# Linear attention with a router on one core: the recurrence's small matmuls in one burst for both sequences, sums of squares later, gates in two steps, the last tile in halves

## The chip, the core and the metric

The kernel runs on one core of a Trainium2 chip. The core has five engines that run on their own, each with a queue that it works off in order: TensorE (PE) multiplies matrices into PSUM, VectorE (DVE), ScalarE (ACT) and GpSimd (POOL) work on tiles, and SyncE (SP) issues most of the DMA transfers. PE's weight loads (loads of the operand that stays in the array) have a row of their own in the profile, PEld. PSUM has eight banks per partition; one bank holds 512 float32 values. The metric is the device time of one execution in microseconds.

## The reference

The input x has 4 sequences of 512 tokens with 512 features. It is normalised and goes two ways.

```
xn = layernorm(x)
# s: attention without softmax, 16 heads of 128, in blocks of tokens
q, k, v = silu(xn @ w_qkv)
kv      = decay * kv + (k * k_decay)^T @ v           # a state per head
o       = (q * q_decay) @ kv + ((q @ k^T) * mask) @ v
s       = (sigmoid(xn @ w_gate) * norm_w * o * rsqrt(mean(o*o) + eps)) @ w_out
# g: softmax router over 64 experts, the 8 largest weights
g       = silu(xn * sum(top8) + top8 @ expert_bias)
out     = x + s * g
```

The mean of o*o runs over all 16 heads (2048 values) of a token.

## The kernel before

**Products.** All large products are float32 products made of three passes over a high and a low part of each operand (`PASSES`): ACT casts the high part, POOL or DVE subtracts it to get the low part. Each matmul has a 128x128 stationary tile and 512 moving columns. The head products (q, k and gates) of two sequences at a time use a scheme with seven block products instead of eight (`unit`, lines 478 to 516). So a *unit* has seven steps of six matmuls. Behind each step come its additions on DVE, the sigmoid on ACT, a product on DVE that is put off to the next step (`deferred`), and then all that the list `after[i]` holds for step i. These lists are how the order of the work is written: nothing is scheduled by a tool.

**Stages.** First the v products (lines 919 to 971), stored to DRAM. Then 48 units in two passes over pairs of sequences (p = 0, 1; `todo`, from line 1005): for each two heads a gate unit, then the q and k unit of either head. Last the output projection (from line 1071): 64 steps, one for each sequence and head, of 12 matmuls (4 token tiles, 3 passes), accumulated over the 16 heads in four PSUM banks `po`.

**The recurrence.** A head's attention runs in the unit after its q and k unit, for the pair's two sequences b1 and b0 (`attention`, line 717). It has three parts, all made of small float32 matmuls (each is one or two records of 128 columns in the trace):

- `scores_qk` (line 660): scores `sa` = k q, transposed k `kt`; then DVE masks the scores (`at`), ACT scales k (`kd`) and POOL scales q (`qd`).
- `states` (line 684): `ss` = kd v, then ACT copies the first block and DVE adds the running state (`st`).
- `attend` (line 697): `o` from at v and qd st; DVE makes y = o * norm_w * gate and SP stores it; ACT squares o, and POOL adds the squares over the heads into `sqs`.

Before, these stand behind the steps one sequence at a time: scores of b1 behind step 1, of b0 behind step 2, states behind 3 and 4, output of b1 behind 5, and of b0 behind step 0 of the next unit. The outputs use two pools of PSUM: `ps_o` (one bank) for b1, `ps_sc` (three banks, for all that is small) for b0. The last unit's k for b0 is the last of four results of a unit; its product with the sigmoid is put off to step 0 of the next unit.

**Routing.** From unit 3 on, the router's small steps (`routing`, line 339) are dealt out one to a step, seven in a unit. Most of them are DVE operations.

**Around the projection.** `sum_squares` (line 726) sums `sqs` over partitions with matmuls of one column, then POOL raises to -1/2. For the first pair it stands behind step 4 of a unit in the second pass; for the second pair, behind step 3 of the projection. The last head's attention runs at steps 0 to 2 of the projection (`last_steps`, line 1058). `ahead` (line 982) loads y and w_out some steps ahead and splits them two or three steps ahead, at the start of every step. `ffn` (line 752) makes the router's gate for one token tile: DVE normalises x, PE multiplies the top-8 weights by the bias (`pu`), then DVE adds, ACT takes the sigmoid and POOL multiplies. `finish` (line 788) multiplies the projection by the norm and the gate, adds x, and stores.

Of the kernel before, what the change touches and what calls it, by code (L numbers as in the profile page):

```python
# [8 lines left out]
F32 = mybir.dt.float32  # L9
# [5 lines left out]
P = 128  # L15
NH = 16
# [34 lines left out]
def kernel(  # L51
# [44 lines left out]
    def tok(b, t):  # L96
        return bass.ds(b * N + t * P, P)
# [443 lines left out]
    def nothing():  # L541
        return [[] for _ in PRODUCTS]
# [114 lines left out]

    def scores_qk(b, h, attp):  # L660
        s, d = (b, h), dec[b // PB, h]
        q, k = chunks(qs[s]), chunks(ks[s])
        pa = ps_sc.tile([P, NT, P], F32, tag="sc", name=f"sa_{b}_{h}")
        for c in range(NT):
            nc.tensor.matmul(pa[:, c], k[:, c], q[:, c], start=True, stop=True)  # L665
        pk = ps_sc.tile([P, NT - 1, P], F32, tag="sc", name=f"kt_{b}_{h}")
        for c in range(NT - 1):
            nc.tensor.transpose(pk[:, c], k[:, c], ident)  # L668
        at[s] = attp.tile([P, NT, P], F32, tag="at", name=f"at_{b}_{h}")
        nc.vector.tensor_tensor(  # L670
            at[s], pa, d[:, 0, None, :].to_broadcast([P, NT, P]), ALU.mult
        )
        kd[s] = attp.tile([P, NT - 1, P], F32, tag="kd", name=f"kd_{b}_{h}")
        nc.scalar.activation(kd[s], pk, AF.Copy, scale=kdecay[:, h : h + 1])  # L674
        qd[s] = attp.tile([P, NT - 1, P], F32, tag="qd", name=f"qd_{b}_{h}")
        nc.gpsimd.tensor_tensor(  # L676
            qd[s], q[:, 1:], d[:, 1, None, :].to_broadcast([P, NT - 1, P]), ALU.mult
        )
# [18 lines left out]
    def attend(b, h, attp, psum=(ps_o, "o")):  # L697
        s = (b, h)
        po = psum[0].tile([P, N], F32, tag=psum[1], name=f"o_{b}_{h}")
        for c in range(NT):  # L700
            o = chunks(po)[:, c]
            nc.tensor.matmul(o, v_of(b, h, c), at[s][:, c], start=True, stop=(c == 0))  # L702
            if c > 0:
                nc.tensor.matmul(o, st[s][:, c - 1], qd[s][:, c - 1], start=False, stop=True)  # L704
        y = attp.tile([P, N], F32, tag="y", name=f"y_{b}_{h}")
        nc.vector.scalar_tensor_tensor(y, po, nw[:, h : h + 1], gts[s], ALU.mult, ALU.mult)  # L706
        nc.sync.dma_start(out=y_d[s], in_=y)
        if h == 0:
            sq[b] = attp.tile([P, N], F32, tag="sqs", name=f"sqs_{b}")
            nc.scalar.activation(sq[b], po, AF.Square)  # L710
        else:
            s1 = attp.tile([P, N], F32, tag="sqt", name=f"sq_{b}_{h}", bufs=1)
            nc.scalar.activation(s1, po, AF.Square)  # L713
            nc.gpsimd.tensor_tensor(sq[b], sq[b], s1, ALU.add)  # L714


    def attention(p, h, attp):
        b0, b1 = p * PB, p * PB + 1
        f = lambda g, b: [lambda: g(b, h, attp)]
        now = [  # L720
            [], f(scores_qk, b1), f(scores_qk, b0), f(states, b1), f(states, b0), f(attend, b1), [],
        ]
        return now, [lambda: attend(b0, h, attp, (ps_sc, "sc"))]


    def sum_squares(b):
# [25 lines left out]
    def ffn(b, t, outp):  # L752
        u = outp.tile([P, F], F32, tag="u", name=f"u_{b}_{t}")
        normalise(u, xts[b, t], b, t)
        pu = ps_sc.tile([P, F], F32, tag="sc", name=f"pu_{b}_{t}")
        for i in range(2):
            nc.tensor.matmul(pu, wT[b][:, t, :], ebs[0][:, i, :], start=(i == 0), stop=(i == 1))  # L757
        nc.vector.scalar_tensor_tensor(u, u, sumw[b][:, t : t + 1], pu, ALU.mult, ALU.add)
        sg = wk.tile([P, F], F32, tag="sg", name=f"sgu_{b}_{t}")
        nc.scalar.activation(sg, u, AF.Sigmoid)  # L760
        nc.gpsimd.tensor_tensor(u, u, sg, ALU.mult)  # L761
        gates[b, t] = u
# [22 lines left out]
        split_lo(nc.gpsimd, wr[:, 1], w, wr[:, 0])  # L785
        wos[h] = wr

    def finish(b, t, ps):
        u, xt = gates[b, t], xts[b, t]
        last = b == B - 1  # L790
        nc.vector.scalar_tensor_tensor(u, ps, rms[b][:, t : t + 1], u, ALU.mult, ALU.mult)  # L791
        (nc.vector if last else nc.gpsimd).tensor_tensor(u, u, xt, ALU.add)
        (nc.scalar if last and t % 2 else nc.sync).dma_start(out=out[tok(b, t), :], in_=u)

    def o_head(pos, h, yr, t):
        for n, (wi, yi) in enumerate(PASSES):
            nc.tensor.matmul(  # L797
                pos[t], yr[:, yi, bass.ts(t, P)], wos[h][:, wi],
                start=(h == 0 and n == 0), stop=(h == NH - 1 and n == len(PASSES) - 1),
            )  # L800


# [202 lines left out]
    for i, (p, kind, n, w) in enumerate(todo):  # L1005
        after = nothing()
        for j, f in enumerate(later):
            after[min(4 * j, 6)].append(f)
        later = []
        if i + 2 < len(todo):  # L1010
            todo[i + 2][3].load()()
        if i + 1 < len(todo):
            weight_steps(todo[i + 1][3], after)
        if pending is not None:
            now, later = attention(*pending, attp)
            for j, fs in enumerate(now):
                after[j] += fs
            if pending[1] == NH - 1:
                later.append(lambda: [sum_squares(b) for b in range(PB)])
            pending = None  # L1020
        if i >= 3:
            for j in range(len(PRODUCTS)):
                if route_steps and (len(route_steps) > 1 or j):
                    after[j].append(route_steps.pop(0))
        if nu - len(XN) + NX <= i < nu:
            if xc is None:
                rb_stack.close()
                xc = right(ha_stack, "xc")
            m = i - (nu - len(XN) + NX)
            block(1, m, xc, m)  # L1030
            load_block(1, m)
        if i == nu - 1:
            for m in range(NX):
                def again(m=m):
                    block(1, len(XN) - NX + m, xa, m)
                    load_block(1, len(XN) - NX + m)
                after[m].append(again)
        if i == nu:
            xb_stack.close()
            op = left(o_stack, "o", 2)  # L1040
        if i == len(todo) - 1:
            ahead(0, 2, 0)
            after[3].append(lambda: ahead(0, 2, 1))
            after[5].append(lambda: ahead(0, 3, 2))
        if kind == "g":
            gate_unit(p, n, w, attp, after)
        else:
            qk_unit(p, n, w, attp, after)
            pending = (p, n)
            if n + 1 < NH or p + 1 < NP:  # L1050
                nxt = (p, n + 1) if n + 1 < NH else (p + 1, 0)
                load_v(*nxt, attp)
                load_decay(*nxt, attp)
# [5 lines left out]
        [lambda: scores_qk(b1, hl, attp), lambda: scores_qk(b0, hl, attp)],  # L1059
        [lambda: states(b1, hl, attp), lambda: states(b0, hl, attp)],  # L1060
        [lambda: attend(b1, hl, attp), lambda: attend(b0, hl, attp, (ps_sc, "sc"))],
        [lambda: sum_squares(b0), lambda: sum_squares(b1)],
    ]

    late_stack = ExitStack()
# [4 lines left out]
        f()  # L1070
    for i, (b, h) in enumerate(steps):
        last = b == B - 1
        if i == len(last_steps) - 1:
            ha_stack.close()
            hw_stack.close()
            late = right(late_stack, "late", 5)
        if late is None:
            ahead(i, 3, 2)
        else:
            ahead(i, 6, 3)  # L1080
        if h == 0:
            for t in range(NT):
                pos[t] = ps_mm.tile([P, F], F32, tag="mm", name=f"po_{b}_{t}")
        if not last or h < NH - TAIL:
            yr = parts.pop(0)
            for t in range(NT):
                o_head(pos, h, yr, t)
                if h == NH - 1:
                    finish(b, t, pos[t])
        elif h == NH - 1:  # L1090
            for t in range(NT):
                for k, yr in enumerate(parts[0:TAIL]):
                    o_head(pos, NH - TAIL + k, yr, t)
                finish(b, t, pos[t])
        if i < len(last_steps):
            for f in last_steps[i]:
                f()
        if late is not None:
            if i == 3:
                load_eb(late)  # L1100
            if i == 5:
                split_eb(late)
            m = h - (4 if b == 0 else 0)
            if m == 0:
                load_wT(b, late)
            if 0 <= m < NT:
                load_x(late, b, m)
            if m in (3, 5, 7, 9):
                ffn(b, (m - 3) // 2, late)
    late_stack.close()  # L1110
    o_stack.close()

# [42 lines left out]
```

## Time and profile before

| | us |
|---|---|
| median of 3 runs | 1075.56 (1074.61 to 1075.66) |
| profiled execution, its own time | 1074.7 |
| its span, first to last instruction | 1073.0 |
| PE busy, 5762 matmuls | 1058.8 |
| PEld busy | 909.6 |
| POOL busy | 724.2 |
| DVE busy | 686.3 |
| ACT busy | 479.8 |

The largest groups of PE are the head products (line 496), the projection (line 797: 768 matmuls, 180.0 us busy) and the small matmuls of the recurrence (lines 665 to 704). The mean granted clock of PE is 0.998.

How to read it: the busy time of PE counts overlapping matmuls once, and the end of a matmul is modelled, so 99% does not say that the array works at its peak. Better is the time from the start of one matmul to the start of the next. In the timelines, a row gives the start in us from the span's start, the duration in us, the engine, the line, the operation, output<-inputs, the number of instructions merged into the row, and in brackets the idle time of the engine ahead of it with what ended it. In the list of waits a row gives who waited for whom, the total in us, how many times, and the longest.

### The profile page before, as it was taken

How to read it: one execution, taken by the hardware profiler on the slowest of the kernel's cores; microseconds unless marked ns; L12 is line 12 of the kernel's file. 1: busy time of each engine (PE TensorE's matmuls, PEld its weight loads, DVE VectorE, ACT ScalarE, POOL GpSimd, SP SyncE). 2: the span in 40 equal slices, each digit the busy share in tenths (PEclk: the TensorE clock that was granted, in tenths of full speed). 3: DMA queues.
4: the chain of work that ended last, by engine and by line, in shares of the span. 5: the costliest groups of instructions: out<-in, count | busy, mean ns of one | idle time of the engine just before them, and what ended most of it. 6: DMA issues, size and time to landing. Idle time of an engine off the chain costs nothing.

```text
span 1073.0 us, 16479 instructions
## 1 busy us (share of the span) xinstructions
PE 1058.8 (99%) x5762; PEld 909.6 (85%) x5762; DVE 686.3 (64%) x1059; ACT 479.8 (45%) x938; POOL 724.2 (67%) x725
## 2 busy tenths in 40 slices
PE   8999999999999999999999999999999999999998
PEld 7788788888888888888888888888888888788886
DVE  5898876667787565655755656556556565854554
ACT  7545545544444444444444444444444444331311
POOL 6898793867768677776786777767877757612130
PEclk9999999999999999999999999999999999999999
DMA  8556745422432223235722232233222428355351
GB/s 276 185 185 243 267 148 177 148 84 95 128 94 94 86 91 109 84 123 176 270 85 72 87 118 84 84 115 97 84 75 90 132 79 275 100 175 176 109 182 55
DMA packets 105059, 143.09 MB, mean 133 GB/s; under 512 B 9104, under 2 KB 53264, under 8 KB 104080
## 3 DMA queue, kind: packets, MB, share of 16 engines
q1 hardware_dynamic: 104112, 141.33, 39.9%
q8 instruction: 46, 0.75, 0.3%
q10 hardware_dynamic: 864, 0.70, 0.2%
q14 instruction: 37, 0.30, 0.1%
HBM read 91.14 MB, written 50.86 MB: 132 GB/s over the span
## 4 chain that ended last, share of the span: by engine, by line
PE 91%; DVE 5%; ACT 2%; DMA 1%; issue 1%; POOL 0%; SPq 0%; DVEq 0%; ACTq 0%; POOLq 0%
PE u_qk L496 27%; PE po L797 16%; PE u_g L496 14%; PE u_v L496 11%; PE sa L665 5%; PE o L702 5%; PE ss L688 4%; PE o L704 4%; PE kt L668 2%; DMA raw_v<-in_w_v_dram 1%; DVE vo_v L552 1%; PE lg L314 1%; PE pu L757 1%; DVE sum_v L432 1%; ACT w_A_v L100 0%
## 5 line engine op out<-in xcount | busy, mean ns | idle before, releaser
L797 PE MATMUL po<-wr,yr 128*128 128x512 f32 x768 | 180.0, 392 | 1.4 <-DVE u L791 1.4
L797 PEld LDWEIGHTS po<-wr,yr 128*128 128x128 f32 x768 | 144.8, 189 | 32.0 <-ACT yr L100 1.8
L496 PE MATMUL u_qk<-blk_T,ws_qk 128*128 128x512 f32 x576 | 149.1, 398 | 0.0
L714 POOL TENSOR_TENSOR sqs<-sqs,sq 128x512 f32<-128x512 f32 x60 | 77.2, 1287 | 90.3 <-ACT sq L713 86.7
L496 PEld LDWEIGHTS u_qk<-blk_T,ws_qk 128*128 128x128 f32 x576 | 104.7, 188 | 20.3
L692 DVE SCALAR_TENSOR_TENSOR st<-st,bdecay,ss 128x128 f32<-128x128 f32 x128 | 44.5, 348 | 105.2 <-ACT st L690 102.9
L496 PE MATMUL u_qk<-blk_B,wa_qk 128*128 128x512 f32 x384 | 99.6, 395 | 0.0
L103 DVE TENSOR_TENSOR yr<-yin,yr 128x512 fp32r<-128x512 f32 x64 | 68.7, 1109 | 46.5 <-ACT yr L100 46.5
L103 POOL TENSOR_TENSOR ws_qk<-sum_qk,ws_qk 128x512 fp32r<-128x512 f32 x64 | 88.4, 1392 | 14.7 <-ACT ws_qk L100 14.6
L702 PE MATMUL o<-at,vin 128*128 128x128 f32 x512 | 88.2, 274 | 0.0
L496 PEld LDWEIGHTS u_qk<-blk_B,wa_qk 128*128 128x128 f32 x384 | 70.8, 188 | 14.3
L702 PEld LDWEIGHTS o<-at,vin 128*128 128x128 f32 x512 | 77.2, 191 | 5.0
L496 PE MATMUL u_g<-blk_T,ws_g 128*128 128x512 f32 x288 | 77.8, 406 | 0.0
L674 ACT ACTIVATE kd<-kt,kdecay 128x384 f32<-128x384 f32 x64 | 37.3, 583 | 87.3 <-PE kt L668 87.3
L704 PE MATMUL o<-qd,st 128*128 128x128 f32 x384 | 74.2, 275 | 0.0
L665 PEld LDWEIGHTS sa<-q,k 128*128 128x128 f32 x512 | 66.6, 191 | 7.9 <-DVE q L552 2.7
L706 DVE SCALAR_TENSOR_TENSOR y<-o,nw,gt 128x512 f32<-128x512 f32 x64 | 47.9, 748 | 39.3 <-PE o L704 38.5
L549 ACT ACTIVATE sg_k<-k 128x512 f32<-128x512 f32 x64 | 40.5, 632 | 65.9 <-DVE k L487 65.9
L761 POOL TENSOR_TENSOR u<-u,sgu 128x512 f32<-128x512 f32 x16 | 20.7, 1292 | 72.6 <-ACT sgu L760 59.9
L665 PE MATMUL sa<-q,k 128*128 128x128 f32 x512 | 67.8, 275 | 1.7 <-DVE q L552 1.6
L676 POOL TENSOR_TENSOR qd<-q,dec 128x384 f32<-128x384 f32 x64 | 65.5, 1024 | 0.0
L496 PE MATMUL u_v<-w_S_v,blk_T 128*128 128x512 f32 x252 | 62.7, 392 | 1.3 <-DVE a_v L487 1.2
(182 smaller groups left out, 2424.3 us busy)
## 6 DMA issues: line engine op xcount, KB each, us to landing
v<-vo_v SPq DMA_DIRECT2D x64, 256.0 KB, 2.1
raw_qk<-in_w_head_dram SPq DMA_DIRECT2D x64, 256.0 KB, 4.0
vin<-v SPq DMA_DIRECT2D x64, 256.0 KB, 3.3
y<-y SPq DMA_DIRECT2D x64, 256.0 KB, 2.3
yin<-y SPq DMA_DIRECT2D x64, 256.0 KB, 3.9
x<-in_x_dram SPq DMA_DIRECT2D x32, 256.0 KB, 4.9
raw_g<-in_w_head_dram SPq DMA_DIRECT2D x32, 256.0 KB, 3.1
raw_v<-in_w_v_dram SPq DMA_DIRECT2D x16, 256.0 KB, 6.2
```

The costliest lines, as they stand in the source:

```text
L103: eng.tensor_tensor(lo, src, hi.bitcast(F32), ALU.subtract)
L496: nc.tensor.matmul(ps, lhsT, rhs, start=(first and c == 0 and n == 0), stop=(c == KC - 1 and n == len(PASSES) - 1), skip_group_check=not f ...
L549: nc.scalar.activation(sg, src, AF.Sigmoid)
L665: nc.tensor.matmul(pa[:, c], k[:, c], q[:, c], start=True, stop=True)
L676: nc.gpsimd.tensor_tensor(qd[s], q[:, 1:], d[:, 1, None, :].to_broadcast([P, NT - 1, P]), ALU.mult)
L688: nc.tensor.matmul(ps[:, c], kd[s][:, c], v_of(b, h, c), start=True, stop=True)
L692: nc.vector.scalar_tensor_tensor(r[:, c], r[:, c - 1], bdecay[:, h : h + 1], ps[:, c], ALU.mult, ALU.add)
L702: nc.tensor.matmul(o, v_of(b, h, c), at[s][:, c], start=True, stop=(c == 0))
L704: nc.tensor.matmul(o, st[s][:, c - 1], qd[s][:, c - 1], start=False, stop=True)
L706: nc.vector.scalar_tensor_tensor(y, po, nw[:, h : h + 1], gts[s], ALU.mult, ALU.mult)
L714: nc.gpsimd.tensor_tensor(sq[b], sq[b], s1, ALU.add)
L797: nc.tensor.matmul(pos[t], yr[:, yi, bass.ts(t, P)], wos[h][:, wi], start=(h == 0 and n == 0), stop=(h == NH - 1 and n == len(PASSES) - 1),)
```

## The change

- **Recurrence.** Both sequences' scores now stand together behind step 1, both states behind step 3, both outputs behind step 6. The transposed k of b0 uses the `ps_o` bank, so that the four score tiles need only three of `ps_sc`. Nothing but the first pair's sums is carried to the next unit, and that goes behind step 5.
- **Routing.** Its steps are dealt out behind steps 1 to 4 alone.
- **Sums of squares.** The tile `sqs` lies in the pool `wk`, which lives to the end; the second pair's sums run at steps 7 and 9 of the projection, one sequence at a time, instead of both at step 3.
- **Projection.** At the last head of each sequence, `ahead` comes behind the results instead of ahead of them. For the first sequence, the loads for the gates and the gates themselves come one step earlier.
- **Gates.** `ffn` ends with the matmuls; the add, sigmoid and product follow a step later in `silu_gate`.
- **Last tile.** The last token tile of the last sequence is done in two halves of 256 columns, each with its own nine matmuls, result and store.

```diff
-    def scores_qk(b, h, attp):
+    def scores_qk(b, h, attp, psum=(ps_sc, "sc")):
...
-        pk = ps_sc.tile([P, NT - 1, P], F32, tag="sc", name=f"kt_{b}_{h}")
+        pk = psum[0].tile([P, NT - 1, P], F32, tag=psum[1], name=f"kt_{b}_{h}")
...
-            sq[b] = attp.tile([P, N], F32, tag="sqs", name=f"sqs_{b}")
+            sq[b] = wk.tile([P, N], F32, tag="sqs", name=f"sqs_{b}")
...
-        f = lambda g, b: [lambda: g(b, h, attp)]
-        now = [
-            [], f(scores_qk, b1), f(scores_qk, b0), f(states, b1), f(states, b0), f(attend, b1), [],
+        now = nothing()
+        now[1] = [
+            lambda: scores_qk(b1, h, attp), lambda: scores_qk(b0, h, attp, (ps_o, "o")),
         ]
-        return now, [lambda: attend(b0, h, attp, (ps_sc, "sc"))]
+        now[3] = [lambda: states(b1, h, attp), lambda: states(b0, h, attp)]
+        now[6] = [lambda: attend(b1, h, attp), lambda: attend(b0, h, attp, (ps_sc, "sc"))]
+        return now
...
+        gates[b, t] = u, pu
+
+    def silu_gate(b, t):
+        u, pu = gates[b, t]
         nc.vector.scalar_tensor_tensor(u, u, sumw[b][:, t : t + 1], pu, ALU.mult, ALU.add)
...
-    def finish(b, t, ps):
-        u, xt = gates[b, t], xts[b, t]
+    def finish(b, t, ps, c=slice(None)):
+        u, xt = gates[b, t][:, c], xts[b, t][:, c]
...
-    def o_head(pos, h, yr, t):
+    def o_head(pos, h, yr, t, c=slice(None), stops=(NH - 1,)):
...
-                pos[t], yr[:, yi, bass.ts(t, P)], wos[h][:, wi],
+                pos[t][:, c], yr[:, yi, bass.ts(t, P)], wos[h][:, wi, c],
...
-            after[min(4 * j, 6)].append(f)
+            after[5].append(f)
...
-                if route_steps and (len(route_steps) > 1 or j):
+                if route_steps and 1 <= j <= 4:
...
-        [lambda: sum_squares(b0), lambda: sum_squares(b1)],
     ]
...
-        if late is None:
-            ahead(i, 3, 2)
-        else:
-            ahead(i, 6, 3)
+        if h < NH - 1:
+            ahead(i, *((3, 2) if late is None else (6, 3)))
...
-                for k, yr in enumerate(parts[0:TAIL]):
-                    o_head(pos, NH - TAIL + k, yr, t)
-                finish(b, t, pos[t])
+                for c in (slice(None),) if t < NT - 1 else (slice(0, F // 2), slice(F // 2, F)):
+                    for k, yr in enumerate(parts[0:TAIL]):
+                        o_head(pos, NH - TAIL + k, yr, t, c)
+                    finish(b, t, pos[t], c)
+        if h == NH - 1:
+            ahead(i, 6, 3)
...
+        if i in (7, 9):
+            sum_squares((b0, b1)[(i - 7) // 2])
...
-            m = h - (4 if b == 0 else 0)
+            m = h - (3 if b == 0 else 0)
...
             if m in (3, 5, 7, 9):
                 ffn(b, (m - 3) // 2, late)
+            if m in (4, 6, 8, 10):
+                silu_gate(b, (m - 4) // 2)
```

More of the change, by code (lines that the diff above doesn't have):

```diff
@@ L786, in split_wo @@
         wos[h] = wr
-    def finish(b, t, ps):
-        u, xt = gates[b, t], xts[b, t]
+    def finish(b, t, ps, c=slice(None)):
+        u, xt = gates[b, t][:, c], xts[b, t][:, c]
         last = b == B - 1
-        nc.vector.scalar_tensor_tensor(u, ps, rms[b][:, t : t + 1], u, ALU.mult, ALU.mult)
+        nc.vector.scalar_tensor_tensor(u, ps[:, c], rms[b][:, t : t + 1], u, ALU.mult, ALU.mult)
         (nc.vector if last else nc.gpsimd).tensor_tensor(u, u, xt, ALU.add)
-        (nc.scalar if last and t % 2 else nc.sync).dma_start(out=out[tok(b, t), :], in_=u)
-    def o_head(pos, h, yr, t):
+        (nc.scalar if last and t % 2 else nc.sync).dma_start(out=out[tok(b, t), c], in_=u)
+    def o_head(pos, h, yr, t, c=slice(None), stops=(NH - 1,)):
         for n, (wi, yi) in enumerate(PASSES):
             nc.tensor.matmul(
-                pos[t], yr[:, yi, bass.ts(t, P)], wos[h][:, wi],
-                start=(h == 0 and n == 0), stop=(h == NH - 1 and n == len(PASSES) - 1),
+                pos[t][:, c], yr[:, yi, bass.ts(t, P)], wos[h][:, wi, c],
+                start=(h == 0 and n == 0), stop=(h in stops and n == len(PASSES) - 1),
+                skip_group_check=c != slice(None),
             )
@@ L1014 @@
         if pending is not None:
-            now, later = attention(*pending, attp)
-            for j, fs in enumerate(now):
+            for j, fs in enumerate(attention(*pending, attp)):
                 after[j] += fs
@@ L1072 @@
         last = b == B - 1
-        if i == len(last_steps) - 1:
+        if i == len(last_steps):
             ha_stack.close()
@@ L1086 @@
             for t in range(NT):
-                o_head(pos, h, yr, t)
+                o_head(pos, h, yr, t, stops=(NH - 1, NH - TAIL - 1) if last and t == NT - 1 else (NH - 1,))
                 if h == NH - 1:
```

## The prediction

> **What bounds it.** I read the engines' busy shares first, then the waits of TensorE (PE), then the timelines of one recurrent step and of the start of the output projection.
>
> ```profile
> PE 1058.8 (99%) x5762; PEld 909.6 (85%) x5762; DVE 686.3 (64%) x1059; ACT 479.8 (45%) x938; POOL 724.2 (67%) x725
> ```
>
> PE is the bound: 99% busy, 91% of the chain of waits. A change can win only what PE loses in gaps, so its waits come next (total, times, longest, in us):
>
> ```profile
> PE sa L665 <- DVE q L552: 1.6, 2, 0.9
> PE po L797 <- DVE u L791: 1.4, 1, 1.4
> ...
> PE ssq L729 <- POOL sqs L714: 0.6, 1, 0.6
> ```
>
> Behind the first phase there is little else to win. One loss isn't a wait. The table by stage (columns: length, busy time and count of PE, PEld, DVE, ACT, POOL, then granted clock, DMA share, GB/s) shows it:
>
> ```profile
> 891.60:895.00 3.40, 2.80 (x21) 2.47 (x21) 2.13 (x4) 1.63 (x3) 2.72 (x3) 1.00 0.80 258
> 895.00:898.40 3.40, 3.40 (x10) 2.62 (x9) 0.88 (x2) 2.05 (x4) 3.40 (x4) 0.51 1.01 358
> ```
>
> Behind the sums of squares PE ran at half clock for 3.4 us: 10 matmuls where 15 fit.
>
> **Edit 1, bursts.** A step's six 512-column matmuls take 1.36 us (514.38 to 515.74 below), 227 ns each. A small record takes 111.5 ns. From the starts of single records, a burst costs beyond these: scores (11 records) 2 ns, states (6) 9, outputs (14) 10. The last head already runs pairs in one burst: states 6 ns for 12 records, outputs 9 for 28. A pair saves 2 + (2x9 - 6) + (2x10 - 9) = 25 ns; 31 pairs save **0.75 us**. Going from one kind of matmul to the other is nearly free here.
>
> **Edit 1, the new deadline.** The second sequence's scores start right behind the first's, a step (1.47 us) earlier than now. PE, then DVE, then POOL, around one even head:
>
> ```profile
> 514.38 1.52 PE L496 MATMUL u_qk<-blk_T,ws_qk 128*128 128x512 f32 x6
> 515.74 1.05 PE L665 MATMUL sa<-q,k 128*128 128x128 f32 x8
> 516.63 0.49 PE L668 MATMUL kt<-ident,k 128*128 128x128 f32 x3
> 516.88 1.63 PE L496 MATMUL u_qk<-blk_T,ws_qk 128*128 128x512 f32 x6
> 518.35 1.05 PE L665 MATMUL sa<-q,k 128*128 128x128 f32 x8
> ```
>
> ```profile
> 512.54 1.27 DVE L552 TENSOR_TENSOR k<-k,sg_k 128x512 f32<-128x512 f32 x1
> ...
> 514.33 1.18 DVE L552 TENSOR_TENSOR q<-q,sg_q 128x512 f32<-128x512 f32 x1
> 515.43 1.22 DVE L552 TENSOR_TENSOR k<-k,sg_k 128x512 f32<-128x512 f32 x1
> ```
>
> ```profile
> 511.95 3.01 POOL L103 TENSOR_TENSOR ws_qk<-sum_qk,ws_qk 128x512 fp32r<-128x512 f32 x2
> 514.93 1.19 POOL L103 TENSOR_TENSOR wb_qk<-raw_qk,wb_qk 128x256 fp32r<-128x256 f32 x1
> 516.07 1.18 POOL L432 TENSOR_TENSOR sum_g<-raw_g 128x256 f32<-128x256 f32 x1
> ```
>
> The last k is ready at 516.65; its scores start at 518.35 now, at 516.97 then. The cover shrinks from 1.70 to 0.32 us. Over all heads: 2.5 us or more left on most odd ones (least 0.75), 0.24 to 0.33 on nearly all the 16 even ones, -0.6 on one. k is the stationary operand, so its weight load (PEld mean 191 ns) comes out of the 0.32 too. I take **0**, ends 0 and 0.5 us for each of some 15 pairs.
>
> It may not stay 0.32: these products take 0.68 us where POOL is idle and 1.2 beside a POOL operation, and POOL's phase moves. On even heads its queue now starts with the add of squares ending near 507.8; with both outputs behind step 6 I work out 507.0. ws's second half is then held by its ACT cast (511.76 to 512.37), begins about 0.1 us ahead of the k product at 512.54, and could hold it 0.5 us longer than now. That is the main rival.
>
> **What else is queued.** Both y products and squares stand ahead of the last k product on odd heads, which have 2.5 us of cover; s1 of the next step waits for the second square on ACT, about as now. qd runs twice ahead of the weight split on POOL: 1.03 us later, for weights used 8 us on. On SP the loads of v, decays and raw weights come behind the second y store (4 us); raw lands 4.0 us after issue and is used a unit, over 11 us, later. PSUM: the next pair's third score tile needs the bank of the last output some 2.4 us after its reads end. The first pair's sums move by one product, and the tiles of squares to another pool of SBUF. All cost 0. Without that cover a late weight load would stop PE for as long as it is late.
>
> **Routing.** Its steps now fall on products 1 to 4, four in a unit instead of seven. Three even heads lose 0.04, 1.04 and 0.84 us now, with some 0.1 us each to refill: 2.2. With one DVE step left at product 4 of even heads (best 0.46, total 0.6, keep 0.6, the low half 0.9 us, less the 0.1 to 0.2 us free and the 0.2 of cover) I get 1.6. **Gain 0.6**, ends 2.2 and -1.
>
> **Start of the output projection.** The last pair's second scores wait 0.26 us for the bank of the previous output (876.96 + 0.60 on ACT), with refill 0.36: gone. Then PE, and POOL:
>
> ```profile
> 892.40 1.95 PE L729 MATMUL ssq<-ones,sqs 128*128 128x1 f32 x16 [0.60 <-POOL sqs L714]
> 894.21 12.75 PE L797 MATMUL po<-wr,yr 128*128 128x512 f32 x48
> ```
>
> ```profile
> 891.07 1.28 POOL L714 TENSOR_TENSOR sqs<-sqs,sq 128x512 f32<-128x512 f32 x1 [0.71 <-ACT sq L713]
> 892.30 1.72 POOL L103 TENSOR_TENSOR wr<-woin,wr 128x512 fp32r<-128x512 f32 x1
> ```
>
> Without the sums, step 4 is reached at 891.2, but its third matmul reads the low half of wr that POOL ends at 894.02, so 893.65 with the 0.36. **A new wait of 2 us takes the place of the old one**; against 894.66 now, 1.0 us is won. The half clock, 1.6 us, goes if 2 us of waiting doesn't bring it back. The sums come later, 2 x 0.95. Then the first gate matmul, one step earlier, needs the split expert bias: its loads land 6.8 us after issue at 894.2, while DMA is full (share 1.01); its cast started at 901.62 and POOL ended it at 903.60, so 903.2 then, and PE is there at 901.4: wait 1.8. Step 10 now starts at 913.15; then 903.4 + three steps 8.16 + a gate 0.45 + sums 1.9 = 913.9. **Loss 0.7 for the group**, ends -1.1 (bias early) and +2.4 (half clock again).
>
> Here a rule is to be weighed. The Trainium skill ("TensorE: Matmul & The Clock Gate", What's actually happening) says the clock is cut after an idle window of some 3.4 us. The rows differ: it fell with PE never idle for 0.9 us, behind 1.8 us of one-column matmuls; another sixteen of them without a wait, in the first pair, did not cut it. By the rule my two waits are harmless; by the rows 23% of dense work in a window is too little and 47% enough, and the first wait leaves 44% at worst. I side with no cut, and keep +1.7 as an end.
>
> **First sequence's end.** Two splits (929.25, 1.98 us) stand on DVE ahead of the first result, and PE waits: 1.84 us from matmul to matmul instead of 0.23, with refill 1.7. With results first, the wait goes. The split for the step after next then ends about 932.4 to 933.0, is needed at 933.1; the y loads behind the output stores on SP (POOL's four adds, 5.94 us) keep over 1 us. **Gain 1.7**, low end 1.4.
>
> **Gates in two steps.** DVE waits 12.5 us for pu in all and ACT 63.3 us for u; neither holds PE. 0.
>
> **Last tile.** Eighteen matmuls of 256 columns replace nine of 512: 18 x 113 to 120 = 2.0 to 2.2 us against 2.04 (bound above: the PEld length 188 each, +1.3). Free overlap would save 0.3 on each of the two DVE operations (0.75 and 0.69) less 0.1: 0.55. Against it speaks the skill's page "PSUM — Partial Sum Buffer" (PSUM bank collisions raise a hardware error): no two engines on one bank at once. Our row for it: ACT's squares wait 57.9 us in 43 times for DVE's y, though both only read. If DVE's read of the first half must end before PE goes on, some 0.6 is given back: **+0.1**; by free overlap -0.55. I take the guarded one.
>
> **Sum.** -0.75 - 0.6 + 0.7 - 1.7 + 0.1 = -2.25 us. The profiled execution took 1074.7 (span 1073.0): 1072.4. It lies 0.9 under the median of the runs, 1075.56, from which the sum gives 1073.3. I say **1073.0**. Within 0.2% (2.15 us) counts as no change, and the sum lies right at that edge.
>
> **Rivals.**
> - *The last k is late on even heads* (slower side). For: 0.32 us of cover, deciding from 0.15 us lateness on (15 x 0.15 eats the sum), slower beyond 0.30. Against: POOL may as well lose the race, and then k is earlier. With 0.2 us, 1076; with 0.35 and 0.1 refill, 15 x 0.45 = 6.8: 1080. Chance 0.30.
> - *The projection's start loses more*: half clock again behind the new wait. 1074.7. Chance 0.12.
> - *Halves overlap and routing waits vanish*: -2.25 - 0.65 - 1.6: 1070.6. Chance 0.08.
> - My sum: 0.50, its own range 1071.5 to 1074.7.
>
> Faster: 0.31 of my sum's half and 0.08 = 0.39. Slower: 0.20 of the k rival, 0.05 of the others = 0.25. The rest 0.36. Range 1071.0 to 1079.5.
>
> **What would show it.** No wait of sa on even heads, or one of 0.1 to 0.5 us on each, with k products near 1.2 or 1.8 us; ssq without a wait; a PE wait for POOL's wr near 892 and for ebs near 902; the clock row at 1.00 or 0.5 there; no wait of po for u near 930; the last tile's second half starting behind DVE or not. I am wrong if the bursts themselves shorten PE by several us, or if waits grow on odd heads.

## The result and the profile after

| | before | after |
|---|---|---|
| median, us | 1075.13 (1074.05 to 1076.06, 6 runs) | 1069.76 (1069.0 to 1071.35, 6 runs) |
| profiled execution, own time | 1074.7 | 1069.32 |
| its span | 1073.0 | 1067.6 |

The ratio is 0.9956, with a 95% interval of 0.9946 to 0.9966: faster by 5.4 us. The prediction said 1073.0, and 1071.0 at the lowest. To see where the rest came from, I set the same marks in both traces. Each row is the length of the stretch up to its mark, after less before:

| mark (start of, us) | before | after | difference | predicted |
|---|---|---|---|---|
| first `sa` of the first head | 212.50 | 212.32 | -0.2 | 0 |
| first `sa` of the last head | 876.13 | 870.97 | **-5.0** | **-1.35** |
| first matmul of the projection's step 10 | 913.15 | 908.76 | +0.8 | +0.7 |
| first gate matmul of the second sequence | 943.05 | 937.18 | -1.5 | -1.7 |
| last gate matmul | 1051.39 | 1045.55 | 0.0 | 0 |
| end of the span | 1073.0 | 1067.6 | +0.45 | +0.1 |

The miss lies in one row, the recurrence. First the busy row of after and the head of its list of waits of PE (total us, times, longest):

```profile
PE 1055.7 (99%) x5771; PEld 910.0 (85%) x5771; DVE 691.3 (65%) x1061; ACT 482.3 (45%) x938; POOL 731.0 (68%) x725
```

```profile
PE po L805 <- DVE u L798: 1.0, 1, 1.0
PE pu L759 <- POOL ebs L103: 0.9, 1, 0.9
PE po L805 <- POOL wr L103: 0.6, 1, 0.6
```

The two waits of `sa` for q (1.6 us), the wait for `u` at the end of the first sequence (1.4) and the one of `ssq` (0.6) are gone. The `u` of this list is another one, in the last tile. In place of the sums' wait stand two new ones at the projection's start. Timeline of PE there:

```profile
886.55 0.51 PE L805 MATMUL po<-wr,yr 128*128 128x512 f32 x1 [0.26 <-ACT wr L100]
887.44 0.50 PE L805 MATMUL po<-wr,yr 128*128 128x512 f32 x1 [0.38 <-DVE yr L103]
888.57 8.01 PE L805 MATMUL po<-wr,yr 128*128 128x512 f32 x34 [0.63 <-POOL wr L103]
896.73 0.50 PE L759 MATMUL pu<-ebs,wTin 128*128 128x512 f32 x1 [0.15 <-ACT ebs L100]
898.08 0.50 PE L759 MATMUL pu<-ebs,wTin 128*128 128x512 f32 x1 [0.85 <-POOL ebs L103]
```

Step 4 waits for the weights' split: from matmul to matmul 0.42, 0.66 and 0.90 us, 1.99 in all, as forecast (2 us). The bias costs 0.31 and 1.13 (1.8 in the forecast). The granted clock stayed at 1.00 here. The waits in brackets are shorter than the delays, since a matmul's modelled end lies behind the next one's start.

In the recurrence, DVE and then POOL at the same even head as shown of before:

```profile
509.16 1.75 DVE L552 TENSOR_TENSOR k<-k,sg_k 128x512 f32<-128x512 f32 x1
510.84 0.68 DVE L487 TENSOR_TENSOR k<-u_qk,a_qk 128x512 f32<-128x512 f32 x1
511.44 0.68 DVE L552 TENSOR_TENSOR q<-q,sg_q 128x512 f32<-128x512 f32 x1
512.28 0.98 DVE L552 TENSOR_TENSOR k<-k,sg_k 128x512 f32<-128x512 f32 x1 [0.16 <-ACT sg_k L549]
```

```profile
507.69 2.68 POOL L103 TENSOR_TENSOR ws_qk<-sum_qk,ws_qk 128x512 fp32r<-128x512 f32 x2
510.35 1.17 POOL L103 TENSOR_TENSOR wb_qk<-raw_qk,wb_qk 128x256 fp32r<-128x256 f32 x1
511.48 1.23 POOL L432 TENSOR_TENSOR sum_g<-raw_g 128x256 f32<-128x256 f32 x1
```

The feared race did take place, and POOL won it: the first k product took 1.75 us instead of 1.27, and ended at 510.91, behind ws's second half at 510.37. But then POOL's next subtraction was nearly over when q's product began, which took 0.68 us instead of 1.18. POOL was not idle beside it: its next addition began 0.04 us later and took 1.23 us. The last k is ready at 513.26, and PE's timeline shows its scores at 513.59:

```profile
512.37 1.05 PE L665 MATMUL sa<-q,k 128*128 128x128 f32 x8
513.26 0.49 PE L668 MATMUL kt<-ident,k 128*128 128x128 f32 x3
513.59 1.06 PE L665 MATMUL sa<-q,k 128*128 128x128 f32 x8
514.48 0.49 PE L668 MATMUL kt<-ident,k 128*128 128x128 f32 x3
514.73 1.64 PE L496 MATMUL u_qk<-blk_T,ws_qk 128*128 128x512 f32 x6
516.20 1.53 PE L496 MATMUL u_qk<-blk_B,wa_qk 128*128 128x512 f32 x6
517.57 1.50 PE L688 MATMUL ss<-vin,kd 128*128 128x128 f32 x12
```

Cover 0.33 us, where 0.32 was forecast. One head waited for k (14 of the second pair, 0.35 us).

The last rows also show what comes next: the step right behind the burst takes 1.47 us (514.73 to 516.20), the one behind that 1.37.

### The profile page after: what moved, and what is told of

Its sections match the earlier page's. It is cut to its first block, busy times and chain, and to the rows that moved or that the text cites. A ratio compares the mean times of both kernels' runs of the same rounds, so it can differ in the third digit from the quotient of the medians.

```text
span 1067.6 us, 16505 instructions
## 1 busy us (share of the span) xinstructions
PE 1055.7 (99%) x5771; PEld 910.0 (85%) x5771; DVE 691.3 (65%) x1061; ACT 482.3 (45%) x938; POOL 731.0 (68%) x725
## 4 chain that ended last, share of the span: by engine, by line
PE 92%; DVE 3%; DMA 2%; ACT 1%; issue 1%; SPq 1%; POOL 0%; DVEq 0%; ACTq 0%; POOLq 0%
PE u_qk L496 28%; PE po L805 15%; PE u_g L496 14%; PE u_v L496 11%; PE o L702 5%; PE sa L665 5%; PE o L704 4%; PE ss L688 4%; PE kt L668 2%; DMA raw_v<-in_w_v_dram 1%; PE lg L314 1%; DVE vo_v L552 1%; PE pu L759 1%; DMA raw_eb<-in_expert_b_dram 1%; DVE sum_v L432 1%
## 5 line engine op out<-in xcount | busy, mean ns | idle before, releaser
L805 PE MATMUL po<-wr,yr 128*128 128x512 f32 (+1 forms) x777 | 179.7, 388 | 2.2 <-DVE u L798 1.0
L103 POOL TENSOR_TENSOR ws_qk<-sum_qk,ws_qk 128x512 fp32r<-128x512 f32 x64 | 82.9, 1297 | 30.4 <-ACT ws_qk L100 29.4
L552 DVE TENSOR_TENSOR k<-k,sg_k 128x512 f32<-128x512 f32 x64 | 90.8, 1418 | 2.4 <-ACT sg_k L549 2.2
L692 DVE SCALAR_TENSOR_TENSOR st<-st,bdecay,ss 128x128 f32<-128x128 f32 x128 | 41.7, 346 | 60.7 <-ACT st L690 58.4
L702 PEld LDWEIGHTS o<-at,vin 128*128 128x128 f32 x512 | 74.9, 191 | 2.5
L103 POOL TENSOR_TENSOR ws_g<-sum_g,ws_g 128x512 fp32r<-128x512 f32 x32 | 42.7, 1334 | 46.4 <-ACT ws_g L100 46.4
L713 ACT ACTIVATE sq<-o 128x512 f32<-128x512 f32 x60 | 35.9, 598 | 72.3 <-POOL sqs L714 43.5
L665 PEld LDWEIGHTS sa<-q,k 128*128 128x128 f32 x512 | 64.3, 191 | 3.5 <-DVE q L552 0.7
```

The lines of the kernel that those rows point to most:

```text
L103: eng.tensor_tensor(lo, src, hi.bitcast(F32), ALU.subtract)
L552: nc.vector.tensor_tensor(dst, src, sg, ALU.mult)
L692: nc.vector.scalar_tensor_tensor(r[:, c], r[:, c - 1], bdecay[:, h : h + 1], ps[:, c], ALU.mult, ALU.add)
L805: nc.tensor.matmul(pos[t][:, c], yr[:, yi, bass.ts(t, P)], wos[h][:, wi, c], start=(h == 0 and n == 0), stop=(h in stops and n == len(PASS ...
```

## The experiments

**Theory**: a burst of small matmuls costs PE more than I had counted, and 93 fewer of them are most of the gain. **Rivals**: the recurrence gains by fewer waits (routing, the order of the steps), or the gain lies in the sums that left step 3 and the half clock behind them. Ratios are to before on the same chip. After was not timed again beside these runs, so a difference from after is one of medians from two times and, in brackets, one of the two ratios (after's is 0.9956).

**One sequence at a time.** The version after with the recurrence dealt out as before.

```diff
-        now[1] = [
-            lambda: scores_qk(b1, h, attp), lambda: scores_qk(b0, h, attp, (ps_o, "o")),
-        ]
-        now[3] = [lambda: states(b1, h, attp), lambda: states(b0, h, attp)]
-        now[6] = [lambda: attend(b1, h, attp), lambda: attend(b0, h, attp, (ps_sc, "sc"))]
-        return now
+        f = lambda g, b: [lambda: g(b, h, attp)]
+        now = [
+            [], f(scores_qk, b1), f(scores_qk, b0), f(states, b1), f(states, b0), f(attend, b1), [],
+        ]
+        return now, [lambda: attend(b0, h, attp, (ps_sc, "sc"))]
...
```

> The changed kernel with the recurrence again one sequence at a time (six bursts a head pair instead of three), all else as changed. Theory (a change from small to large matmuls costs some 42 ns, because about ten matmuls behind a burst start 3 to 10 ns late each; 93 bursts more): 3.9 us slower than the changed kernel, about 1073.7, with no new waits of PE in the recurrence. Rival (bursts nearly free, 25 ns a pair, as I predicted; the gain is from waits that went): 0.8 us slower, about 1070.5.

Measured: 1073.98 us, ratio 0.9989 (0.9981 to 0.9997).

**Bursts alone.** The version before with nothing but the reverse of that edit.

> The kernel before with the bursts alone (scores, states and outputs of both sequences together; routing, sums, gates and last tile as before). Theory (42 ns a burst): 3.9 us faster than before, about 1071.2. Rival (25 ns a pair): 0.8 us faster, about 1074.3; it is slower than before if the waits for routing grow with the earlier scores.

Measured: 1070.76, ratio 0.9966 (0.9952 to 0.998). Both ways round the bursts are worth about four: 4.2 us out of after (3.5 by the ratios), 4.5 into before (3.7; median of before in those runs 1075.25). All other parts of the change together are worth 1.3 us in the first of the two runs.

The trace of bursts alone says where. The first `sa` of the first and of the last head:

```profile
212.40 0.72 PE L665 MATMUL sa<-q,k 128*128 128x128 f32 x5
...
872.09 0.72 PE L665 MATMUL sa<-q,k 128*128 128x128 f32 x5
```

The recurrence takes 659.69 us, where before took 663.63: 3.9 us less. What is left of this run's gain is the sum of two differences that have little to do with bursts: the projection's start is 2.0 us shorter, as this execution shows no half clock, and the end of the first sequence 1.4 longer.

And where in the recurrence? I took a stretch that no wait disturbs: from the scores of head 2 to those of head 14 in the second pair, 18 units, 756 large and 744 small records in each trace. The first row of the scores at either end, before, then after, then one at a time:

```profile
603.08 0.72 PE L665 MATMUL sa<-q,k 128*128 128x128 f32 x5
...
859.53 0.94 PE L665 MATMUL sa<-q,k 128*128 128x128 f32 x7
```

```profile
599.13 0.94 PE L665 MATMUL sa<-q,k 128*128 128x128 f32 x7
...
854.07 1.05 PE L665 MATMUL sa<-q,k 128*128 128x128 f32 x8
```

```profile
602.14 0.83 PE L665 MATMUL sa<-q,k 128*128 128x128 f32 x6
...
858.65 0.83 PE L665 MATMUL sa<-q,k 128*128 128x128 f32 x6
```

The stretch takes 256.45 us before, 254.94 after, 256.51 one at a time, and 254.93 with bursts alone. So 36 bursts fewer are 1.51 us, 126 ns for the three of a pair, and 31 pairs make **3.9 us**. The same stretch says where: I gave each record the time from its start to the next one's, took off the beat (226.7 ns for a large, 111.5 for a small one), and summed from each burst to the next:

```
ns per burst   one by one (before)   both in one burst (after)   saved by a pair
scores               17.3                     16.6                     18
states               26.8                     14.6                     39
outputs              43.8                     18.4                     69
```

For the single bursts, most of this stands behind the second large matmul, where my count of 2, 9 and 10 ns stopped: up to the tenth behind a burst, most take 228 to 236 ns on the mean instead of 227 (one takes 224). A step of six takes 1.47 us behind a burst, and 1.36 on the beat; the burst's own last record gives 81 ns back.

**States apart.** Twelve bursts more in that stretch, all else as after.

```diff
-        now[3] = [lambda: states(b1, h, attp), lambda: states(b0, h, attp)]
+        now[3] = [lambda: states(b1, h, attp)]
+        now[4] = [lambda: states(b0, h, attp)]
```

> The changed kernel with the two states apart, b1 behind step 3 and b0 behind step 4: 31 bursts more. Theory (42 ns a burst): 1.3 us slower than the changed kernel, about 1071.1, a third of what the full undoing costs. Rival (12 ns, the part of a burst that ends with its first large matmul): 0.4 us, 1070.1.

Measured: 1072.3 (1069.78 to 1073.07, a wide range), ratio 0.9971 (0.996 to 0.9983). The stretch takes 255.67, 0.73 more: 61 ns for each burst added. The sum per kind gives 37.5 ns for one states burst here, so a pair costs 2 x 37.5 - 14.6 = 60 more. The same single burst cost 26.8 in before: its price depends on its neighbours. One head of this run, from the second states burst to the outputs:

```profile
606.68 0.83 PE L688 MATMUL ss<-vin,kd 128*128 128x128 f32 x6
607.26 1.63 PE L496 MATMUL u_qk<-blk_B,ws_qk 128*128 128x512 f32 x6
608.73 1.54 PE L496 MATMUL u_qk<-blk_T,wb_qk 128*128 128x512 f32 x6
610.11 0.61 PE L702 MATMUL o<-at,vin 128*128 128x128 f32 x4
```

The first step behind the burst takes 1.47 us, and the second is still late, 1.38 for 1.36. On the mean of the 12 heads, the burst of b1, with one step of six large matmuls ahead of the next burst, costs 30 ns, and that of b0, with two such steps, 46. The single outputs of before do the same: 31 ns with one step behind them, 47 with two. A burst that comes soon cuts off the tail of the one ahead of it.

**More bursts, more records.** After, with one or with four transposes of the identity into an unread bank added behind step 4 of each of the 48 units, where no burst stands.

```diff
+    def extra():
+        ps = ps_sc.tile([P, P], F32, tag="sc", name="extra")
+        for _ in range(1):
+            nc.tensor.transpose(ps, ident, ident)
...
+        after[4].append(extra)
```

> The changed kernel with one small transpose (one record, into a bank that nobody reads) added behind step 4 of each of the 48 units: 48 more bursts of one record. Together with the run of four transposes it gives the price of a burst apart from its records (a record is 0.1115 us). Theory (some 42 ns a burst): 48 x (0.1115 + 0.042) = 7.4 us slower than the changed kernel, about 1077. Rival (a burst is nearly free, 10 ns): 5.8 us, 1075.5.

> The same with four transposes in a burst behind step 4 of each unit. Theory: 48 x (0.446 + 0.042) = 23.4 us slower than the changed kernel, about 1093; the part that does not grow with the number of records is 2.0 us. Rival: 21.9 us, and that part 0.5 us.

Measured: 1075.88 with one (ratio 1.0011, 1.0004 to 1.0017), 1091.17 with four (1.0154, 1.0141 to 1.0168). In the stretch one adds 2.46 us and four add 8.50, over 18 units. The three more records are 6.04 us, 112 ns each, which is the beat; what is left is (2.46 - 18 x 0.112) / 18 = 25 ns for the burst. Over the whole run one adds 6.1 us to the median of after, 127 ns a unit, and four add 21.4: that is less burst than the stretch shows, and no more than records at the beat in the second. Both lie nearer to the rival's forecast than to the theory's, so 42 ns is no general price. It went from 25 to 61 ns for one burst more, by kind and place. The steps behind a burst are one part of that, but not all: in the run of four, the extra bursts cost 18 ns in 12 of the 18 units and 42 in the other 6, though two steps or more stand behind each. Why stays open.

**Routing in seven steps.** After, with the router's steps dealt out as before.

```diff
-                if route_steps and 1 <= j <= 4:
+                if route_steps and (len(route_steps) > 1 or j):
```

> The changed kernel with routing dealt out again one to every step, seven in a unit. Theory (the waits of PE for the last k and q come from DVE's routing steps at products 4 to 6 and 0): waits of about 1 us come back on two or three even heads, and the scores' second half meets them too: 1.9 to 2.5 us slower than the changed kernel, 1071.7 to 1072.3. Rival (routing's place is worth nothing, the waits went with the order of the outputs): 1069.8, no such waits.

Measured: 1071.93, ratio 0.9971 (0.9959 to 0.9982), 2.2 us over after (1.6). Its undisturbed stretch is that of after (254.94). Of its trace's 2.6 us, 1.0 lies in the recurrence, where matmuls on heads 4 and 6 of the first pair start 0.66, 0.44 and 0.82 us behind the one before. Another 1.0 lies in the projection's start, where the bias came later (delays of 1.27 and 1.13 us, for 0.31 and 1.13 in after). So the theory's forecast of 1.9 to 2.5 us was met by luck: only 1.0 us of it is routing's. From its list of waits:

```profile
PE pu L759 <- ACT ebs L100: 1.1, 1, 1.1
PE pu L759 <- POOL ebs L103: 0.8, 1, 0.8
```

So routing is worth about 1.0 us of the recurrence's 5.0, and the bursts 3.9, which is also what the run of bursts alone shows. The bias's arrival differs from trace to trace whatever was edited; how much of the spread of the untraced executions that is, is not shown.

**Sums at step 3.** After, with the second pair's sums where they were.

```diff
-        if i in (7, 9):
-            sum_squares((b0, b1)[(i - 7) // 2])
+        if i == 3:
+            sum_squares(b0)
+            sum_squares(b1)
```

> The changed kernel with both sums of squares behind step 3 of the projection again, the tiles of squares still in the pool that lives on. Theory (moved later they left a wait for w_out's low half in their place, and are paid for again at steps 7 and 9, while PE waits for the expert bias in any case): the sums fill the wait at step 4 and the two later ones (1.8 us in all) go: 1.3 to 1.9 us faster, about 1068.2, with a wait of ssq of 0.6 to 0.9 us back. Rival (the wait ahead of the sums and the half clock behind them are worth more than that): 0.5 to 1.5 us slower, 1070.3 to 1071.3, with a granted clock near 0.5 for 3.4 us.

Measured: 1068.79, ratio 0.9942 (0.993 to 0.9955). PE's timeline in the profiled execution:

```profile
886.79 1.95 PE L731 MATMUL ssq<-ones,sqs 128*128 128x1 f32 x16 [0.60 <-POOL sqs L714]
888.60 8.41 PE L805 MATMUL po<-wr,yr 128*128 128x512 f32 x36
896.85 0.84 PE L759 MATMUL pu<-ebs,wTin 128*128 128x512 f32 x2
```

The sums wait again, but behind them PE waits neither for the weights nor, but for 0.1 us, for the bias: at step 3 the 1.8 us of sums fill time that PE otherwise spends waiting. And the half clock did not come back here. So moving the sums was no gain in itself; by the medians it lost 1.0 us (1.5), though the two intervals overlap.

**Gates a step later.** After, with the first sequence's gates at the steps they had before, still in two steps.

```diff
-            m = h - (3 if b == 0 else 0)
+            m = h - (4 if b == 0 else 0)
```

> The changed kernel with the first sequence's gates and their loads of x and weights a step later again, as before the change. Theory (the first gate matmul waits 1.4 us for the split expert bias, whose load lands late because DMA is full): the wait goes, 1.2 to 1.6 us faster than the changed kernel, about 1068.4. Rival (the wait only moves: PE then waits as long for y or w_out, which land behind the bias): no change, 1069.8.

Measured: **1067.61** (1067.46 to 1068.79), ratio 0.9935 (0.9922 to 0.9947). All five executions lie under after's lowest (1069.0); the median is 2.1 us under after's (2.3). The bias is there in time, and one sequence's sums stand in front of it:

```profile
888.47 10.72 PE L805 MATMUL po<-wr,yr 128*128 128x512 f32 x46 [0.63 <-POOL wr L103]
899.03 0.95 PE L731 MATMUL ssq<-ones,sqs 128*128 128x1 f32 x8
899.84 0.71 PE L759 MATMUL pu<-ebs,wTin 128*128 128x512 f32 x2
```

**Splits first.** After, with `ahead` ahead of the results in every step.

```diff
-        if h < NH - 1:
+        if True:
             ahead(i, *((3, 2) if late is None else (6, 3)))
...
-        if h == NH - 1:
-            ahead(i, 6, 3)
```

> The changed kernel with the loads and splits ahead of the results at the last head too, as before the change. Theory (the splits on DVE held up the first result, and PE waited for it at the start of the second sequence): a wait of po for u of 1 to 1.6 us comes back near 925, 1.0 to 1.6 us slower, about 1071.1. Rival (the wait went with the gates in two steps, which free DVE and ACT at that point): no wait, 1069.8; or faster, as the loads no longer stand behind the output stores.

Measured: 1070.42, ratio 0.9961 (0.9947 to 0.9974), 0.7 over after (0.5). DVE at the end of the first sequence, splits first and then after:

```profile
924.52 1.98 DVE L103 TENSOR_TENSOR yr<-yin,yr 128x512 fp32r<-128x512 f32 x2 [1.27 <-ACT yr L100]
926.42 2.71 DVE L798 SCALAR_TENSOR_TENSOR u<-po,rms,u 128x512 f32<-128x512 f32 x4
```

```profile
923.83 1.38 DVE L103 TENSOR_TENSOR yr<-yin,yr 128x512 fp32r<-128x512 f32 x1 [1.27 <-ACT yr L100]
925.14 2.71 DVE L798 SCALAR_TENSOR_TENSOR u<-po,rms,u 128x512 f32<-128x512 f32 x4
```

With splits first, PE's gap is 0.77 us from matmul to matmul instead of 0.23: 0.54 lost, where before lost 1.6. One split stands ahead of the results in after too. So the order alone is a third of this step's gain. I put the rest down to the gates, which come earlier and in two steps; no run takes these two apart.

This run's clock was cut too, behind the 2 us wait at the projection's start. Table by stage, splits first and then after, with the columns explained above:

```profile
886.60:890.00 3.40, 2.12 (x7) 1.04 (x6) 2.42 (x2) 1.79 (x4) 2.57 (x2) 0.99 0.94 289
890.00:893.40 3.40, 3.40 (x9) 2.64 (x8) 1.00 (x2) 2.15 (x4) 2.49 (x2) 0.50 0.92 322
```

```profile
886.50:888.60 2.10, 1.03 (x3) 0.41 (x3) 1.24 (x2) 0.62 (x1) 2.01 (x2) 1.00 0.88 302
888.60:892.00 3.40, 3.40 (x15) 2.83 (x16) 0.94 (x2) 1.80 (x3) 1.29 (x1) 1.00 0.86 303
```

The same wait stands ahead of both: once the clock falls to 0.50, once it stays at 1.00.

**The last tile whole, and a half in between.** After, with the last tile in one piece; then with the halves kept, but the third tile put between them.

```diff
...
-                for c in (slice(None),) if t < NT - 1 else (slice(0, F // 2), slice(F // 2, F)):
+                for c in (slice(None),):
```

```diff
-            for t in range(NT):
-                for c in (slice(None),) if t < NT - 1 else (slice(0, F // 2), slice(F // 2, F)):
+            lo, hi, whole = slice(0, F // 2), slice(F // 2, F), slice(None)
+            for t, c in ((0, whole), (1, whole), (3, lo), (2, whole), (3, hi)):
...
```

> The changed kernel with the last tile whole again. Theory (the second half's matmuls wait 1.0 us for DVE to read the first half, since both lie in one bank; that and the nine matmuls more cost 1.3, the shorter end wins 0.9): 0.4 us faster, about 1069.3, with PE running on without a wait to its last matmul. Rival (the halves win, as the short end is worth more than the wait): 0.5 us slower, 1070.3.

> The changed kernel with the last tile's first half done ahead of the last but one tile, and its second half last. Theory (the wait for the bank is hidden by the nine matmuls of the tile between): the wait of 1.0 us near the end goes, the short end stays: 0.8 to 1.0 us faster, about 1068.9. Rival (DVE, busy with the tile between, is then late for the last half): 0.2 to 0.5 us faster only.

Measured: 1068.91 whole (ratio 0.9944, 0.993 to 0.9958) and 1069.2 in between (0.9949, 0.9936 to 0.9961). Neither median stands clear of after's executions (1069.0 to 1071.35), and the profiled execution of whole was its slowest (1072.57, with the clock halved at 899.5, far ahead of the last tile). So I read the traces from the last gate matmul to the end of the span: before 21.37 us, after 21.83, whole 21.37, in between 20.96. PE and then DVE at the end of after:

```profile
1057.79 3.73 PE L805 MATMUL po<-wr,yr 128*128 128x512 f32 x20
...
1062.48 1.34 PE L805 MATMUL po<-wr,yr 128*128 128x256 f32 x9 [0.96 <-DVE u L798]
```

```profile
1061.95 0.48 DVE L798 SCALAR_TENSOR_TENSOR u<-po,rms,u 128x256 f32<-128x256 f32 x1
1062.46 0.42 DVE L799 TENSOR_TENSOR u<-u,x 128x256 f32<-128x256 f32 x1
1063.85 0.48 DVE L798 SCALAR_TENSOR_TENSOR u<-po,rms,u 128x256 f32<-128x256 f32 x1 [0.97 <-PE po L805]
```

The second half's matmuls start 0.05 us behind the end of DVE's read of the first half, and wait 0.96 us for it: the bank goes from PE to DVE and back. What PE waits for is DVE's semaphore, by the row; whether the two could have overlapped without it, no run shows. With the third tile in between, PE has no wait:

```profile
1057.73 5.50 PE L805 MATMUL po<-wr,yr 128*128 128x512 f32 x32
```

**All three.** Gates a step later, a half in between, and sums at step 3.

> The changed kernel with the sums back at step 3, the first sequence's gates a step later, and the last tile's first half ahead of the last but one tile. Theory: the waits for w_out's low half, for the expert bias and for the last tile's bank all go; 2.7 to 3.0 us faster than the changed kernel, about 1066.9; the first two overlap (either leaves the bias time to land), so it isn't the sum of the three alone. Rival (the gains are partly the same wait, and the half clock comes back behind the sums): 1 to 2 us faster.

Measured: 1067.64 (1066.97 to 1070.28), ratio 0.9939 (0.9927 to 0.9952), 2.1 us under after by the medians (1.8): not the 2.7 to 3.0 of the theory, and no better than gates a step later alone. In the profiled execution the clock was halved at 889.3 for 3.4 us. The interval overlaps after's, so of the two only gates a step later is clear of after.

## Why the prediction was wrong

**The step that failed**: "Edit 1, bursts", and in it the term "A pair saves 2 + (2x9 - 6) + (2x10 - 9) = 25 ns; 31 pairs save 0.75 us". It is the mis-sized term of the sum: a pair saves 126 ns, and 31 save 3.9 us. The sign and the place were right. The count stopped at the second large matmul, and concluded that "going from one kind of matmul to the other is nearly free here". The trace of before held the answer: the undisturbed stretch is 2.1 us longer than its records at the beat, 29 ns for each of its 72 bursts. I had worked from single starts and not set the sum of the stretch against its length. Nor could the list of waits show it, where I looked under "A change can win only what PE loses in gaps": late starts of a few ns stand in no wait. The prediction's own sign of being wrong came true: the bursts themselves shorten PE by several us. With 3.9 for 0.75 the sum is -5.4 us, which is the result; but that it comes out so exactly is partly luck, as the other terms show.

- *Routing*: -0.6 forecast, -1.1 by the recurrence's 5.0 less the bursts' 3.9, with 1.0 in the trace of the run that undoes it. Heads 2, 4 and 6 of the first pair lost 2.2 us in before and nothing in after, where two starts 0.37 and 0.28 us behind the one before instead of 0.23 stand later, near heads 10 and 8. Right in kind, low in size.
- *The new deadline on even heads*: cost 0 forecast; one wait of 0.35 us. The rival did not come. Its mechanism did, POOL won the race, but what the first product lost the second got back. "0.68 us where POOL is idle" was a wrong reading of the condition: the product of 0.68 us ran beside a POOL addition that began behind it.
- *The projection's start*: +0.7 forecast, +0.8 measured, with the new wait at 2.0 of 2.0 us and the bias's at 1.4 of 1.8. That the half clock stays away held in the profiled execution of after, but not for the reason given ("44% at worst", so no cut): with splits first the same three delays, 1.99 us of the 3.40 ahead, leave 41% and were followed by a cut.
- *The first sequence's end*: -1.7 forecast, -1.5 measured. Its cause was only partly right: results first is worth 0.54, not all of it.
- *The last tile*: +0.1 forecast, +0.46 measured. The guarded reading was right for this program: PE and DVE take turns at the bank, and the wait is 1.0 us where 0.6 was put.
- *What else is queued*, and gates in two steps: 0 forecast; nothing of it shows as a wait of PE.

Without the bursts the forecast is -1.5 us; the run that undoes them alone measured -1.3.

## What to carry to other kernels

Before pricing the switches between two kinds of matmul, take a stretch without waits and set its length against records times beat; the rest, divided by the switches, is their price, and it includes the late matmuls that stand far behind a switch. A wait that lies in front of another wait may cost nothing to keep: sums of squares moved out of it came back as work elsewhere. A last tile in halves gained here only when PE had other work while the tile's bank was read.

## What the runs showed of the hardware

- A burst of 128-column matmuls between 512-column ones cost 17 to 44 ns on the mean of its kind in before. Most of it lies in large matmuls up to the tenth behind the burst, most of them at 228 to 236 ns instead of 227. Two bursts joined cost 15 to 18 together in after.
- The half clock came without long idle time: in the profiled executions of before (895.1), of one transpose added (895.2), of the whole tile (899.5), of splits first (890.0) and of all three (889.3), each time for 3.4 us. With splits first it came behind delays of 0.43, 0.66 and 0.90 us from matmul to matmul, with PE busy for 2.12 of the 3.40 us ahead of it. After has the same three delays, and sums at step 3 has the sums where all three has them, and neither was cut. What decides it, these runs do not show.
- A product of two tiles in SBUF on DVE that began while a POOL operation on tiles in SBUF ran ended 0.54 to 0.55 us behind the end of that operation, in all five cases around the even head shown of before and after; it took 0.98 to 1.75 us. The sixth began 0.04 us ahead of POOL's operation and took 0.68.
- A 256-column matmul took 114 to 125 ns from start to start in after, about half a 512-column one (227) and little over a 128-column one (111.5).
